# A hand-scheduled scan, attention and expert kernel: larger steps for the side work, a smaller pace for the experts, and a folded weight product two banks at a time

## The chip, the cores and the metric

The kernel runs on one core of a Trainium2 chip. The metric is the device time of one execution in microseconds (us), the median of several runs. The engines are named PE (TensorE), DVE (VectorE), ACT (ScalarE), POOL (GpSimd) and SP (SyncE, which issues nearly all DMAs here).

## The reference

Four images of 384 channels and 32 by 32 pixels, all float32. Layer 0 is a selective state-space scan after a group norm; layer 1 is causal attention and a mixture of four experts.

```python
x = x + L0(_gn(x))                 # group norm, projections, scan, norm, gelu
t = _to_tokens(x)                  # (4, 1024, 384)
t = t + attn(_ln_t(t), Wq, Wk, Wv) # causal, one head of 384
t = t + ffn(_ln_t(t), ...)         # gate; every expert 384 -> 1536 -> 384, top 2 kept

# in L0, for each of 4 directions, 384 channels, 16 states, over 1024 positions:
dA = jnp.exp(dtt[..., None] * A)
h = h * dA + (dtt * ut)[..., None] * bt[:, :, None, :]
y = jnp.einsum('bkdn,bkn->bkd', h, ct)

# in attn:
wei = softmax(where(causal, q @ k.T * scale, -inf));  out = wei @ v
```

## The kernel before

**Ticks.** The scan is cut into 768 units, 192 an image, each of 128 rows (32 channels by 4 states) and 1024 positions. The program is written out by hand as a loop over ticks, one unit a tick: ACT makes the decay `da` (`decay`, L554), DVE the product `v` (`front`, L561) and the scan `h` (`middle`, L567), POOL multiplies `h` by the output row (`back`, L584), and every fourth tick PE sums four units over their states into `y` with eight matmuls (`row`, L609). Each engine takes its instructions strictly in the order of this loop; there is no other scheduler.

**Work beside the scan.** Everything else is in generators that yield when they want to go on: `("wait", n)` is n ticks later, `("pe", n)` says that matmuls worth n units have been issued, `("inner", 0)` asks to be continued in the next tick ahead of its scan (`unpark`). At the end of every tick `go_on` (L1376) deals out TensorE time:

- `spare` grows by `pace` a tick, at most to `pace`.
- Every generator of the list `side` is stepped with a budget of 1.0. It goes on until its budget is used up or it waits, so a step that issues more than 1.0 ends its turn. What it used is taken from `spare`.
- What is left goes to the first generator of `waiting`, as long as `spare` is positive.

`side` holds `fold` (once, from tick 192), `finish` (the norm, gelu and sum that end layer 0 of an image), `ready` (the norm and the gates ahead of the experts, for each half image) and `skip`. `waiting` holds `behind(b)`, one for each image: it waits for `finish(b)`, then runs `attention` at a pace of 4.4 and `experts` at a pace of 3.3. So while image b + 1 is scanned, image b's attention and experts run on PE. `preparation(b)` (group norm, projections `pxd` and `pdt` to the step sizes, and `du` on DVE, L441) runs ahead of it, a step of 1.0 a tick.

**The pieces that the change touches.** `layernorm` (L639 on) issues the mean matmuls `mu` (L652), subtracts on DVE (L660), squares on ACT, sums with `var` (L679), takes the root on ACT (L687) and the reciprocal on DVE (L692), spreads it with `rb` (L698) and multiplies on DVE (L708). `finish` calls it with 1024 columns (tiles `..._l0`), `ready` with 512 (`..._ff`). `scaled_tokens` is attention's own norm (`var_at`, `rs_at`, `rb_at`, result `axn`). `fold` makes, from the weights, the centred product of query and key (`pwt`, `pg`) and the centred value weight (`pwv`), and stores both in DRAM (`g_d`, `wv_d`); `attention` loads them for every image (`wg_`, `wv_`). `experts` issues `ph` (L1272), moved by ACT and put through gelu in place (L1257, L1261), and `fy` (L1297), weighted and summed on DVE (L1306, L1309).

**Buffers.** `banks` are four PSUM banks of 512 columns (two during image 1), `slots` eight SBUF buffers of 4 KB a partition; `take` waits for one in steps of a tick. `pools["ht"]` has two buffers, which `fold`, the attention's `qt` and `vt` and the experts' `ht` share.

Of the kernel before, what the change touches and what calls it, by code (L numbers as in the profile page):

```python
# [8 lines left out]
F32 = mybir.dt.float32  # L9
AF = mybir.ActivationFunctionType  # L10
ALU = mybir.AluOpType
# [4 lines left out]
P = 128  # L16
B = 4
C = 384
M = C // P
HW = 32  # L20
L = HW * HW
# [21 lines left out]
AHEAD = 5  # L43
SLOTS = 8
PACE_A = 4.4
PACE_E = 3.3


@with_exitstack
def hybrid_kernel(  # L50
# [22 lines left out]
    nc = tc.nc  # L73
# [17 lines left out]
    pools = {  # L91
        "st": first.enter_context(tc.tile_pool(name="stp", bufs=2)),
        "v": first.enter_context(tc.tile_pool(name="ps_v", bufs=2, space=PSUM)),
        "pm": ps_m,
    }
# [22 lines left out]
    class Shared:  # L118
# [20 lines left out]
        def give(self, *names):  # L139
# [3 lines left out]
    banks = Shared(  # L143
        FIRST_BANKS,
        lambda i, name: (ps_m if i < FIRST_BANKS else pools["pm"]).tile(
            [P, 512], F32, tag=f"pm{i}", name=name
        ),
        0,
    )
    slots = Shared(  # L150
        SLOTS, lambda i, name, *shape: slotp.tile(list(shape), F32, tag=f"s{i}", name=name), 1
    )
# [7 lines left out]
    ident = const.tile([P, P], F32, tag="ident", name="ident")  # L160
    make_identity(nc, ident)
    mean_w = const.tile([P, P], F32, tag="mean_w", name="mean_w")
# [87 lines left out]
    scale = float(C) ** -0.5  # L250
# [465 lines left out]
    def fold():  # L716

        extra = pools["a0"].tile([P, M, L], F32, tag="a0", name="w_extra")
        extra = extra.rearrange("p m l -> p (m l)")
        vs = extra[:, : 2 * M * C].rearrange("p (j c d) -> p j c d", j=2, c=M)
        centre = extra[:, 2 * M * C : 2 * M * C + 2 * P].rearrange("p (j d) -> p j d", j=2)
        nc.sync.dma_start(vs[:, 0], wv.rearrange("(c p) d -> p c d", p=P))
        for same in range(2):
            nc.vector.scalar_tensor_tensor(
                centre[:, same, :], ident, float(same), mean_w, ALU.mult, ALU.subtract
            )  # L730
        def square(name):
            t = pools["ht"].tile([P, M, L], F32, tag="ht", name=name)
            t = t.rearrange("p m l -> p (m l)")[:, : 2 * M * C]
            return t.rearrange("p (j c d) -> p j c d", j=2, c=M)

        raw = square("w_raw")
        for j, w in enumerate((wq, wk)):
            nc.sync.dma_start(raw[:, j], w.rearrange("(c p) d -> p c d", p=P))
        wt = square("w_t")
        yield "wait", 2  # L740
        for j in range(2):
            for d in range(M):
                ps = yield from banks.take(f"pwt_{j}_{d}")
                for c in range(M):
                    for o in range(M):
                        nc.tensor.matmul(
                            ps[:, c * P : (c + 1) * P], raw[:, j, o, d * P : (d + 1) * P],
                            centre[:, int(o == c), :], start=(o == 0), stop=(o == M - 1),
                        )
                yield "wait", 1  # L750
                nc.scalar.copy(wt[:, j, d, :], ps[:, :C])
                banks.give(f"pwt_{j}_{d}")
        g = square("g_s")[:, 0]
        for m in range(M):
            ps = yield from banks.take(f"pg_{m}")
            for d in range(M):
                nc.tensor.matmul(
                    ps[:, :C], wt[:, 0, d, m * P : (m + 1) * P], wt[:, 1, d, :],
                    start=(d == 0), stop=(d == M - 1),
                )  # L760
            yield "wait", 1
            nc.scalar.activation(g[:, m, :], ps[:, :C], AF.Copy, scale=-scale)
            banks.give(f"pg_{m}")
        yield "wait", 1
        nc.sync.dma_start(g_d, g)
        for m in range(M):
            ps = yield from banks.take(f"pwv_{m}")
            for c in range(M):
                nc.tensor.matmul(
                    ps[:, :C], centre[:, int(c == m), :], vs[:, 0, c, :],  # L770
                    start=(c == 0), stop=(c == M - 1),
                )
            yield "wait", 1
            nc.scalar.copy(vs[:, 1, m, :], ps[:, :C])
            banks.give(f"pwv_{m}")
        yield "wait", 1
        nc.sync.dma_start(wv_d, vs[:, 1])
        folded.append(1)


# [119 lines left out]
    def scaled_tokens(b, yb):  # L900

        sqs = []
        for c in range(M):
            sq = yield from slots.take(f"sq_at_{b}_{c}", P, L)
            nc.scalar.activation(sq, yb[:, c, :], AF.Square)
            sqs.append(sq)

        var = yield from banks.take(f"var_at_{b}")
        for o, src in ((NH * P, [yb[:, c, :] for c in range(M)]), (0, sqs)):
            for h in range(NH):  # L910
                for c in range(M):
                    for q in range(4):
                        k = h * 512 + q * P
                        nc.tensor.matmul(  # L914
                            var[32 * q : 32 * (q + 1), o + h * P : o + (h + 1) * P],
                            mean_w[:, :32], src[c][:, k : k + P],
                            start=(c == 0), stop=(c == M - 1), tile_position=(0, 32 * q),
                        )
                yield "pe", 1.0
        slots.give(*[f"sq_at_{b}_{c}" for c in range(M)])  # L920
        rs = one.tile([P, NH, P], F32, tag=f"rs{NH}", name=f"rs_at_{b}")
        flat = rs.rearrange("p h t -> p (h t)")
        nc.scalar.activation(flat, var[:, NH * P : 2 * NH * P], AF.Square)
        yield "inner", 0
        nc.vector.tensor_tensor(flat, var[:, : NH * P], flat, ALU.subtract)
        banks.give(f"var_at_{b}")
        nc.scalar.activation(rs, rs, AF.Sqrt, bias=eps)
        yield "wait", 1
        nc.vector.reciprocal(rs, rs)
        backs = []  # L930
        for h in range(NH):
            rb = yield from banks.take(f"rb_at_{b}_{h}")
            for q in range(4):
                nc.tensor.matmul(  # L934
                    rb[:, q * P : (q + 1) * P],
                    ident[:, 32 * q : 32 * q + 1].to_broadcast([P, P]), rs[:, h, :],
                    start=True, stop=True,
                )
            backs.append(rb)
            yield "pe", 1.0  # L940
        while b > 0 and b - 1 not in stored:

            yield "wait", 1
        xn = pools["a0"].tile([P, M, L], F32, tag="a0", name=f"axn_{b}")
        yield "inner", 0
        for h in range(NH):
            s = bass.ts(h, 512)
            nc.vector.tensor_tensor(
                xn[:, :, s], yb[:, :, s], backs[h].unsqueeze(1).to_broadcast([P, M, 512]), ALU.mult
            )  # L950
            banks.give(f"rb_at_{b}_{h}")
        return xn

    def attention(b, yb, fx0):

        alone = b == B - 1
        while not folded:
            yield "wait", 1
        gw_ = []
        for name, w in ((f"wg_{b}", g_d), (f"wv_{b}", wv_d)):  # L960
            ta = yield from slots.take(f"{name}a", P, 2, C)
# [1 line left out]
            tb = yield from slots.take(f"{name}b", P, C)  # L963
            nc.sync.dma_start(tb, w[:, 2, :])
            gw_.append((ta[:, 0, :], ta[:, 1, :], tb))
        xn = yield from scaled_tokens(b, yb)
        qt = pools["ht"].tile([P, M, L], F32, tag="ht", name=f"qt_{b}")
        vt = pools["ht"].tile([P, L // P, C], F32, tag="ht", name=f"vt_{b}")

# [384 lines left out]
    def step(g, budget):  # L1354

        if g in ended:
            ended.remove(g)
            return None
        while budget > 0 and until.get(id(g), -100) <= clock[0]:
            try:  # L1360
                what, n = next(g)
            except StopIteration:
                return None
            if what == "pe":
                budget -= n
            elif what == "inner":
                parked.append(g)
                until[id(g)] = clock[0] + 1
            elif what == "start":
                started.append(1)  # L1370
                break
            elif n > 0:
                until[id(g)] = clock[0] + n
        return budget

    def go_on():  # L1376
        spare[0] = min(spare[0] + pace[0], pace[0])
        for g in side[:]:
            left = step(g, 1.0)
            if left is None:  # L1380
                side.remove(g)
            else:
                spare[0] -= 1.0 - left
        while waiting and spare[0] > 0:
            left = step(waiting[0], spare[0])
            if left is None:
                waiting.pop(0)
                continue
            spare[0] = left
            break  # L1390
# [100 lines left out]
```

## Time and profile before

| | |
|---|---|
| median of 3 runs | 3749.89 us (3745.99 to 3752.34) |
| the profiled execution | 3747.14 us, its span 3745.0 us |
| mean granted PE clock | 0.932 |
| PE busy | 3350.6 us (89%) |
| DVE busy | 2961.6 us (79%) |
| ACT busy | 2085.8 us (56%) |
| first and last scan start | 50.3 us, 3078.5 us |

Busy times are shares of the whole span; the stages differ. Matmul records overlap, so that a busy PE need not be a full one. In the tables of waits, a line "DVE du L441 <- PE fy L1297: 15.2, 6, 6.7" says that DVE stood idle ahead of `du` for 15.2 us in 6 places, 6.7 at most, until PE's fy matmuls released it. In the lines by stretch, the columns are the stretch, its length, then busy us (and instructions) of PE, PE weight loads, DVE, ACT and POOL, the granted PE clock, the DMA share and GB/s.

### The profile page before, as it was taken

The page shows a single profiled execution, that of the slowest core. Times are in us where ns is not written, and L with a number is a line of the kernel's source. Part 1 is how long each engine was busy: PE and PEld are TensorE (multiplying, and loading weights), DVE is VectorE, ACT ScalarE, POOL GpSimd, SP SyncE. Part 2 cuts the span into 40 slices and gives each one's busy share as a digit, 9 for nine tenths or more (in the row PEclk, how much of TensorE's full clock was granted, in tenths as well). Part 3 has the DMA queues.
Part 4 walks back from the last instruction along what each step waited for, and adds up shares of the span by engine and source line. Part 5 has one row for each costly group of instructions (what it writes and reads, how often), then busy time and mean ns, then how long its engine had stood idle before and what let it go on. Part 6 is the DMA issues. An engine that isn't in the chain of part 4 may idle for free. (4 is left out here: it accounts for less than half of the span.)

```text
span 3745.0 us, 35189 instructions
## 1 busy us (share of the span) xinstructions
PE 3350.6 (89%) x11891; PEld 1529.0 (41%) x11891; DVE 2961.6 (79%) x2084; ACT 2085.8 (56%) x2832; POOL 1817.8 (49%) x776
## 2 busy tenths in 40 slices
PE   4666667789999999898999999889999998999999
PEld 1333333345333343344333344454344444544444
DVE  5999899988998998989998999999999982210000
ACT  4788888556666555566655555455554552412121
POOL 2777777555565565545555665455665650000000
PEclk7677777899999999999999999899999999999999
DMA  6665666645665756436666665455657551322321
GB/s 204 219 233 199 208 218 221 215 145 199 235 222 201 260 206 230 155 138 228 217 221 229 201 210 192 146 182 188 223 192 240 179 182 38 92 82 83 96 82 53
DMA packets 408019, 680.03 MB, mean 182 GB/s; under 512 B 33520, under 2 KB 279968, under 8 KB 407840
## 3 DMA queue, kind: packets, MB, share of 16 engines
q1 hardware_dynamic: 401632, 677.40, 53.0%
q8 instruction: 94, 1.54, 0.2%
q10 hardware_dynamic: 6208, 0.39, 0.1%
q14 instruction: 85, 0.70, 0.1%
HBM read 605.16 MB, written 72.55 MB: 181 GB/s over the span
## 5 line engine op out<-in xcount | busy, mean ns | idle before, releaser
L584 POOL TENSOR_TENSOR h<-h,bc 128x1024 f32<-128x1024 f32 x768 | 1816.7, 2370 | 1264.9 <-DVE v L561 1058.3
L567 DVE TENSOR_TENSOR_SCAN h<-da,v 128x1024 f32<-128x1024 f32 x768 | 1748.4, 2283 | 48.4 <-PE v L872 17.3
L554 ACT ACTIVATE da<-dt,a 128x1024 f32<-128x1024 f32 x768 | 886.5, 1162 | 868.1 <-DVE h L567 759.3
L1297 PE MATMUL fy<-ht,w 128*128 128x512 f32 x2304 | 1019.8, 599 | 7.5 <-ACT ht L1261 5.9
L1272 PE MATMUL ph<-fx,w 128*128 128x512 f32 x2304 | 1019.1, 598 | 3.8 <-DMA w<-in_w 2.9
L561 DVE TENSOR_TENSOR v<-du,bc 128x1024 f32<-128x1024 f32 x664 | 842.8, 1269 | 61.9 <-DMA du<-dts 25.9
L1297 PEld LDWEIGHTS fy<-ht,w 128*128 128x128 f32 x2304 | 435.6, 191 | 580.3 <-issue 551.0
L1272 PEld LDWEIGHTS ph<-fx,w 128*128 128x128 f32 x2304 | 433.4, 191 | 579.6 <-issue 529.5
L609 PE MATMUL y<-h,sel 128*32 128x512 f32 x3072 | 493.3, 657 | 91.2 <-POOL h L584 89.2
L1257 ACT ACTIVATE ht<-ph,b1s 128x512 f32<-128x512 f32 x384 | 257.9, 679 | 471.0 <-PE ph L1272 469.2
L1306 DVE SCALAR_TENSOR_TENSOR fy<-fy,b2s,tw 128x512 f32<-128x512 f32 x96 | 72.0, 750 | 423.0 <-PE fy L1297 423.0
L609 PEld LDWEIGHTS y<-h,sel 128*32 128x32 f32 x3072 | 96.6, 115 | 399.3 <-issue 220.3
L850 ACT ACTIVATE st<-turn,bt 128x128 f32<-128x128 f32 x832 | 244.2, 554 | 0.0
L872 PE MATMUL v<-ident,st 128*128 128x128 f32 x832 | 147.5, 337 | 86.2 <-DVE h L567 85.4
L1261 ACT ACTIVATE ht<-ht 128x3072 f32<-128x3072 f32 x64 | 176.9, 2764 | 0.8
L872 PEld LDWEIGHTS v<-ident,st 128*128 128x128 f32 x832 | 121.7, 175 | 127.7 <-DVE h L567 74.2
L554 ACT ACT_TABLE_LOAD x99 | 127.0, 1283 | 18.7 <-DMA dt<-dts 12.3
L425 PE MATMUL pdt<-xd,wdt 12*128 12x512 f32 x184 | 88.0, 813 | 45.7 <-ACT dt L433 22.6
L1079 PE MATMUL po<-pt,vt 128*128 128x256 f32 x480 | 102.8, 364 | 7.1 <-ACT pt L971 7.1
L1009 PE MATMUL ss<-axn,qt 128*128 128x512 f32 (+3 forms) x288 | 102.3, 503 | 3.9 <-ACT yb L1096 3.9
L1079 PEld LDWEIGHTS po<-pt,vt 128*128 128x128 f32 x480 | 90.4, 192 | 22.3 <-ACT pt L971 10.1
L1009 PEld LDWEIGHTS ss<-axn,qt 128*128 128x128 f32 x288 | 51.5, 196 | 47.1 <-issue 33.5
(208 smaller groups left out, 1612.3 us busy)
## 6 DMA issues: line engine op xcount, KB each, us to landing
bc<-rows SPq DMA_DIRECT2D x384, 512.0 KB, 4.7
w<-in_w SPq DMA_DIRECT2D x384, 384.0 KB, 6.0
dt<-dts SPq DMA_DIRECT2D x192, 512.0 KB, 4.5
du<-dts SPq DMA_DIRECT2D x192, 512.0 KB, 6.6
dts<-dt SPq DMA_DIRECT2D x48, 512.0 KB, 4.7
dts<-du SPq DMA_DIRECT2D x48, 512.0 KB, 5.3
fx<-t2d SPq DMA_DIRECT2D x12, 768.0 KB, 5.5
tw<-mkd SPq DMA_DIRECT2D x32, 256.0 KB, 6.2
```

The costliest lines, as they stand in the source:

```text
L554: u["decay"] = nc.scalar.activation(u["da"], spread["dt4", n], AF.Exp, scale=a4[:, g, u["q"] : u["q"] + 1])
L561: return nc.vector.tensor_tensor(u["v"], spread["du4", n], spread["bc", n][:, 0, :], ALU.mult)
L567: nc.vector.tensor_tensor_scan(u["h"][:, ::step], u["da"][:, ::step], u["v"][:, ::step], 0.0, op0=ALU.mult, op1=ALU.add,)
L584: product = units[n]["product"] = nc.gpsimd.tensor_tensor(h, h, spread["bc", n][:, 1, :], ALU.mult)
L609: units[n]["row"] = nc.tensor.matmul(y, sel, h, start=first, stop=last, tile_position=(0, jj * DJ))
L850: nc.scalar.activation(st[:, 4 * h + t, :].rearrange("p (d i) -> p i d", i=NI)[:, i, :], ps[h][:, t * P : (t + 1) * P], AF.Copy, scale=bt[ ...
L872: nc.tensor.transpose(u["v"][:, t * P : (t + 1) * P], st[:, t, u["j"] * P : (u["j"] + 1) * P], ident)
L1079: nc.tensor.matmul(pv[:, o:], vt[:, j, m * P : (m + 1) * P], pts[step][j // 4][:, j % 4, o:], start=(alone and j == 0), stop=(j == nj - 1),)
L1257: nc.scalar.activation(ht[:, f, :], ps, AF.Identity, bias=bias)
L1261: nc.scalar.activation(ht, ht, AF.Gelu)
L1272: nc.tensor.matmul(ps, tiles[n][:, c, (f % 2) * P : (f % 2 + 1) * P], xns[h][:, c, :], start=(c == 0), stop=(c == M - 1),)
L1297: nc.tensor.matmul(pss[m], tiles[n][:, f, :], hts[fh][:, f, :], start=(fh == 0 and f == 0), stop=(fh == 1 and f == FH - 1),)
```

## The change

The budget of a side generator's step goes from 1.0 to 3.0, and the experts' pace from 3.3 to 3.2. `fold` keeps its value weight and centring matrices in slots and not in attention's buffer `a0`, issues two banks of matmuls a tick and moves them a tick later, and stores both results at its end. For the first image, `attention` runs `scaled_tokens` before it waits for `fold` and before it loads the weights.

```diff
-PACE_E = 3.3
+PACE_E = 3.2
+BESIDE = 3.0
...
     def fold():
-        extra = pools["a0"].tile([P, M, L], F32, tag="a0", name="w_extra")
...
-        nc.sync.dma_start(vs[:, 0], wv.rearrange("(c p) d -> p c d", p=P))
...
         raw = square("w_raw")
         for j, w in enumerate((wq, wk)):
             nc.sync.dma_start(raw[:, j], w.rearrange("(c p) d -> p c d", p=P))
+        va = yield from slots.take("va", P, 2, C)
+        vb = yield from slots.take("vb", P, C)
+        centre = yield from slots.take("centre", P, 2, P)
+        wvs = wv.rearrange("(c p) d -> p c d", p=P)
+        nc.sync.dma_start(va, wvs[:, :2, :])
+        nc.sync.dma_start(vb, wvs[:, 2, :])
+        vs = (va[:, 0, :], va[:, 1, :], vb)
...
-        yield "wait", 2
-        for j in range(2):
-            for d in range(M):
-                ps = yield from banks.take(f"pwt_{j}_{d}")
-                for c in range(M):
-                    for o in range(M):
-                        nc.tensor.matmul(
-                            ps[:, c * P : (c + 1) * P], raw[:, j, o, d * P : (d + 1) * P],
-                            centre[:, int(o == c), :], start=(o == 0), stop=(o == M - 1),
-                        )
-                yield "wait", 1
-                nc.scalar.copy(wt[:, j, d, :], ps[:, :C])
-                banks.give(f"pwt_{j}_{d}")
-        g = square("g_s")[:, 0]
-        for m in range(M):
-            ps = yield from banks.take(f"pg_{m}")
...
-            yield "wait", 1
-            nc.scalar.activation(g[:, m, :], ps[:, :C], AF.Copy, scale=-scale)
-            banks.give(f"pg_{m}")
-        yield "wait", 1
-        nc.sync.dma_start(g_d, g)
...
+        def by_twos(what, jobs):
+            for n in range(0, len(jobs), 2):
+                some = jobs[n : n + 2]
+                while not banks.ready(len(some)):
+                    yield "wait", 1
+                names = [f"{what}_{n + i}" for i in range(len(some))]
+                moves = [f(banks.now(name)) for f, name in zip(some, names)]
+                yield "wait", 1
+                for move in moves:
+                    move()
+                banks.give(*names)
+
+        yield "wait", 2
+        pairs = [(j, d) for d in range(M) for j in range(2)]
+        yield from by_twos("pwt", [lambda ps, j=j, d=d: turned_weight(j, d, ps) for j, d in pairs])
+        both = square("g_s")
+        jobs = [lambda ps, m=m: product(m, ps) for m in range(M)]
+        yield from by_twos("pg", jobs + [lambda ps, m=m: centred(m, ps) for m in range(M)])
+        slots.give("va", "vb", "centre")
+        nc.sync.dma_start(g_d, both[:, 0])
+        nc.sync.dma_start(wv_d, both[:, 1])
+        yield "wait", 1
         folded.append(1)
...
     def attention(b, yb, fx0):
         alone = b == B - 1
-        while not folded:
-            yield "wait", 1
+        if b == 0:
+            xn = yield from scaled_tokens(b, yb)
+            while not folded:
+                yield "wait", 1
         gw_ = []
...
-        xn = yield from scaled_tokens(b, yb)
+        if b > 0:
+            xn = yield from scaled_tokens(b, yb)
...
         for g in side[:]:
-            left = step(g, 1.0)
+            left = step(g, BESIDE)
             if left is None:
                 side.remove(g)
             else:
-                spare[0] -= 1.0 - left
+                spare[0] -= BESIDE - left
```

More of the change, by code (lines that the diff above doesn't have):

```diff
@@ L716, in fold @@
     def fold():
-        extra = pools["a0"].tile([P, M, L], F32, tag="a0", name="w_extra")
-        extra = extra.rearrange("p m l -> p (m l)")
-        vs = extra[:, : 2 * M * C].rearrange("p (j c d) -> p j c d", j=2, c=M)
-        centre = extra[:, 2 * M * C : 2 * M * C + 2 * P].rearrange("p (j d) -> p j d", j=2)
-        nc.sync.dma_start(vs[:, 0], wv.rearrange("(c p) d -> p c d", p=P))
-        for same in range(2):
-            nc.vector.scalar_tensor_tensor(
-                centre[:, same, :], ident, float(same), mean_w, ALU.mult, ALU.subtract
-            )
         def square(name):
@@ L738, in fold, with turned_weight, product @@
             nc.sync.dma_start(raw[:, j], w.rearrange("(c p) d -> p c d", p=P))
-        wt = square("w_t")
-        yield "wait", 2
-        for j in range(2):
-            for d in range(M):
-                ps = yield from banks.take(f"pwt_{j}_{d}")
-                for c in range(M):
-                    for o in range(M):
-                        nc.tensor.matmul(
-                            ps[:, c * P : (c + 1) * P], raw[:, j, o, d * P : (d + 1) * P],
-                            centre[:, int(o == c), :], start=(o == 0), stop=(o == M - 1),
-                        )
-                yield "wait", 1
-                nc.scalar.copy(wt[:, j, d, :], ps[:, :C])
-                banks.give(f"pwt_{j}_{d}")
-        g = square("g_s")[:, 0]
-        for m in range(M):
-            ps = yield from banks.take(f"pg_{m}")
+        va = yield from slots.take("va", P, 2, C)
[5 more added lines that the diff above has]
+        vs = (va[:, 0, :], va[:, 1, :], vb)
+        for same in range(2):
+            nc.vector.scalar_tensor_tensor(
+                centre[:, same, :], ident, float(same), mean_w, ALU.mult, ALU.subtract
+            )
+        wt = square("w_t")
+        def turned_weight(j, d, ps):
+            for c in range(M):
+                for o in range(M):
+                    nc.tensor.matmul(
+                        ps[:, c * P : (c + 1) * P], raw[:, j, o, d * P : (d + 1) * P],
+                        centre[:, int(o == c), :], start=(o == 0), stop=(o == M - 1),
+                    )
+            return lambda: nc.scalar.copy(wt[:, j, d, :], ps[:, :C])
+        def product(m, ps):
             for d in range(M):
@@ L760, in fold, with centred @@
                 )
-            yield "wait", 1
-            nc.scalar.activation(g[:, m, :], ps[:, :C], AF.Copy, scale=-scale)
-            banks.give(f"pg_{m}")
-        yield "wait", 1
-        nc.sync.dma_start(g_d, g)
-        for m in range(M):
-            ps = yield from banks.take(f"pwv_{m}")
+            return lambda: nc.scalar.activation(both[:, 0, m, :], ps[:, :C], AF.Copy, scale=-scale)
+        def centred(m, ps):
             for c in range(M):
                 nc.tensor.matmul(
-                    ps[:, :C], centre[:, int(c == m), :], vs[:, 0, c, :],
+                    ps[:, :C], centre[:, int(c == m), :], vs[c],
                     start=(c == 0), stop=(c == M - 1),
                 )
-            yield "wait", 1
-            nc.scalar.copy(vs[:, 1, m, :], ps[:, :C])
-            banks.give(f"pwv_{m}")
+            return lambda: nc.scalar.copy(both[:, 1, m, :], ps[:, :C])
+        def by_twos(what, jobs):
[18 more added lines that the diff above has]
+        nc.sync.dma_start(wv_d, both[:, 1])
         yield "wait", 1
-        nc.sync.dma_start(wv_d, vs[:, 1])
         folded.append(1)
@@ L956, in attention @@
         alone = b == B - 1
-        while not folded:
-            yield "wait", 1
+        if b == 0:
+            xn = yield from scaled_tokens(b, yb)
+            while not folded:
+                yield "wait", 1
         gw_ = []
```

## The prediction

> **What bounds the kernel now.** I began with the page's slices: they show two regimes.
>
> ```profile
> PE   4666667789999999898999999889999998999999
> DVE  5999899988998998989998999999999982210000
> PEclk7677777899999999999999999899999999999999
> ```
>
> VectorE is at 9 until slice 32 (the scans end at 3078.5 us), then falls away while TensorE stays at 9. So there are two clocks: the 768 scan ticks, then what TensorE still has to do. Next, busy time by stretch: 80 ticks of the third image's experts, and the gap after the last scan.
>
> ```profile
> 2651.00:2959.00 308.00, 307.77 (x935) 124.04 (x934) 301.30 (x186) 167.70 (x155) 189.10 (x81) 1.00 0.64 216
> 3092.50:3143.90 51.40, 38.69 (x241) 21.86 (x237) 21.71 (x19) 15.01 (x18) 0.00 (x0) 0.87 0.20 69
> ```
>
> First line: VectorE is busy 301.3 of 308 us over 186 instructions, which leaves 36 ns an instruction: no wait, so it sets a tick of 3.85 us. TensorE reads as full too, so the two are nearly balanced. Second line: TensorE has 12.7 us idle in 51.4, and its clock falls to 0.87. Then the waits of VectorE from 675 to 3078 us (images 2 to 4 in the scan):
>
> ```profile
> DVE nb L1026 <- PE ss L1014: 17.0, 7, 9.5
> DVE du L441 <- PE fy L1297: 15.2, 6, 6.7
> DVE v L561 <- PE y L609: 11.1, 9, 3.7
> DVE du L441 <- PE ph L1272: 10.6, 3, 8.9
> DVE du L441 <- ACT dt L433: 5.1, 3, 2.6
> ...
> DVE sc L1130 <- PE pgate L1123: 2.9, 1, 2.9
> DVE red L1145 <- ACT sc L1143: 2.5, 2, 1.6
> DVE axn L948 <- PE rb_at L934: 2.3, 3, 1.1
> DVE rs_l L692 <- ACT rs_l L687: 1.8, 1, 1.8
> DVE rs_at L925 <- ACT rs_at L923: 1.6, 1, 1.6
> DVE fx L660 <- PE mu_ff L652: 1.4, 1, 1.4
> ```
>
> These are what a lighter TensorE can win: 30.9 us for du (the step-size projections that sit behind expert matmuls), 11.1 for the y rows, 18.8 for the row minima nb. Last, the chain that ended last, where image 4's first norm goes over into its attention:
>
> ```profile
> 3126.32 1.14 ACT yb L888
> 3127.49 1.22 DVE yb L893
> ...
> 3131.29 4.54 PE var_at L914 x80
> ...
> 3138.09 1.76 DVE rs_at L929
> 3139.99 2.06 PE rb_at L934 x8
> 3142.07 1.76 DVE axn L948
> 3143.88 15.72 PE pq L980 x36
> ```
>
> Until 3143.88 TensorE waits for the other engines, step by step; from there the chain is nearly all TensorE, to 3745.
>
> **What the Trainium skill says.** "Perfetto Trace Analysis", section "Tensor Engine Instruction (MATMUL, LD_WEIGHTS)": the end of a matmul in a profile is estimated, and VectorE and ScalarE are strict FIFO. The trace agrees on the first: a ph matmul shows 598 ns, while starts lie 429 ns apart, so I price TensorE by starts. The second is why a late TensorE stops the scans: du stands in front of the next scan on VectorE. "ScalarE: Activation LUTs", "What ACT_TABLE_LOAD costs": 1283 ns a table load; the row of 99 loads has the same mean. "TensorE: Matmul & The Clock Gate", "What's actually happening": after an idle window of about 3.4 us the array runs at half speed; the records of var_at above stand 213 ns apart by fours where the layernorm's var stands at 107 elsewhere, after such a gap.
>
> **Prices** (start to start at full clock; each fp32 matmul is two records): 512 columns 0.858 us, 384 columns 0.644, 256 columns 0.43, 128 columns 0.22, the eight y matmuls of a row 2.05, a projection matmul pdt 0.52. A unit of the pace (2.6 for three 512-column matmuls, 2.574 us) is 0.99 us.
>
> **The change part by part.**
>
> *Work moved.* The matmuls are the same. Their order in the changed program, with these prices, gives the TensorE time (before/after, us) of ticks 0-192: 380.5/380.5; 192-256: 232.2/247.8; 256-384: 497.5/489.7; 384-448: 241.2/243.0; 448-576: 495.3/480.6; 576-640: 233.7/233.7; 640-768: 487.7/472.2; after the last row: 626.4/647.0. So 20.6 us leave the scan for the end: 12 ph and 12 fy matmuls of image 3's last expert. The early fold puts 15.6 us more before tick 256, and the smaller pace takes it back by tick 397, where image 1's experts end in both.
>
> *The scan, du and y.* I set the TensorE sum against the VectorE sum (scan 2.28, product 1.27, and so on, each plus 35 ns) four ticks at a time, and carry over what TensorE is late. Summed over the four-tick groups of ticks 256-512 that hold projection matmuls this backlog is 45.0 us before and 26.2 after, 42% less: of 30.9 us of du waits, **-13.1**. Over all groups from tick 192 it is 225 and 157, 30% less: of 11.1 us of y waits, **-3.3**. In the attention stretches it stays (59 and 59), so nb **0**. From tick 640 no such wait is left to win: VectorE sets the tick. Bounds: all 42 us, or nothing.
>
> *New tight handoffs.* With a budget of 3, a side generator goes through its next step in the same tick. In a layernorm one tick of slack goes between var and the reciprocal, one or two between rb and the multiply, and, with 512 columns (ff), one between mu and the subtraction. Behind each waiting VectorE instruction stands the next scan, and behind that GpSimd's product and the row. In the scan there are 3 l0 (2 handoffs) and 6 ff (3): 24. Before has handoffs of such a distance: axn 2.3, rs_at 1.6, sc 2.9, red 2.5, 9.3 us over 18, so 0.52 each; 24 x 0.52 = 12.4, less rs_l and fx mu_ff that it already pays (3.2): **+9.2**. Bounds: 0 (TensorE early every time) and 40 (each waits 1.7, the mean of du and nb being longer).
>
> *The end.* Before, from the end of the last y (3092.5) to pq: 51.4 us. After, by its order: ph 5.1, mu 5.1, ph 2.6, wait for the squares 1.3, var 1.5, square root and 1.75 reciprocal with nothing between 2.5, rb 1.4, ph 2.6, fy 30.9, var_at 2.4 (its inputs are long done, full clock), then the chain to pq as before 8.1: 63.6, so +12.2. The 9 us hole before var_at is filled by fy. Against it: before, TensorE is 6.0 us late at the last row by the sums (the last product ends at 3083.3, y starts at 3090.6); after, 0; I take -5.5. In the ff norms of image 4, rb no longer waits (1.4) but var does (about 2): +0.6. Together **+7.3**. From there 601 us as before.
>
> *Costed at nothing.* Fold's two banks a tick: the ScalarE copies are as many, and TensorE is idle 1.1 us a tick in ticks 192-208, which takes 14.6 us more with 17 to spare; if not, the mu and rb of the first norm wait, a few us. The load of wq and wk goes ahead of wv on SP's queue; still 2 ticks. The loads of the product for image 1 now stand on SP's queue behind var_at (their slots come from it) and in front of pq; between lie a square root, a 1.75 us reciprocal, rb and a multiply, about 8 us at 3131-3144, against 6.0 us to land for a like w load; without that cover 0 to 6 us of TensorE, in a stretch where VectorE sets the time. The three extra slots until tick 201 leave prep its own.
>
> *Sum.* -13.1 - 3.3 + 9.2 + 7.3 = +0.1 on the profiled execution (3747.14, its span 3745.0), which lies 2.8 under the median of the runs, 3749.89. So 3750.
>
> **Rivals.** A measurement of this kernel can tell about 0.2%, 7.5 us, from no change.
> *The stalls go altogether* (faster): with the load at 0.96 of VectorE's instead of 0.98, all but a quarter of du and y goes, -31.5, and handoffs cost 0.2 each, +1.6; with the end's +7.3: -22.6, about 3727. For it: no projection group from 256 to 468 keeps more than 3 us of backlog, tick 412 apart. Against: groups 484 and 500 then hold 6.
> *Handoffs stop the scans* (slower): the bursts put mu and var behind a tick of expert matmuls, 1.5 us a time: 24 x 1.5 - 3.2 = 33, so +24, 3774. It decides from (7.5 + 9.1 + 3.2)/24 = 0.8 us a handoff. For it: nb, emitted one tick after its matmuls, once waited 9.5. Against: at turnovers rows start as soon as their products are there.
> *The pace does nothing* (no change): VectorE sets the tick anyway, so only the end counts, +7.3, 3757.
>
> **How the numbers follow.** The even trade, with the last rival at its edge, 0.36, its own range 3742 to 3757; faster 0.33; slower 0.31. The range 3726 to 3771 takes in the first rival and the slower one up to 1.4 us a handoff.
>
> **What would show it.** After: du <- PE and ACT dt together near 18 us instead of 31; ticks 640-768 no shorter; about 63 us between the last y and pq, with var_at right behind fy; about 9 us more waits at L660, L692, L708's places. Wrong if the scans end more than 15 us earlier or at all later than 3078, or if pq starts less than 8 us later after the last y than before.

## The result, and the profile after

The changed kernel takes **3795.9 us**, median of four runs (3794.5 to 3799.9), against 3750.4 for the kernel before beside it: ratio **1.0122** [1.0109, 1.0135], 45.5 us slower. The forecast was 3750, with a range of 3726 to 3771. The profiled execution is 3796.39 us, its span 3794.6 (before 3745.0: +49.6).

First, of the page's slices of the changed kernel, VectorE and TensorE's granted clock: a digit for each fortieth of the span.

```profile
DVE  6999899897999999978999999999999982210000
PEclk7777777798999999898999999999999999999999
```

VectorE's row has a 7 in slices 10 and 18, where images turn over; before, no slice of the scans but the first was under 8. The clock has an 8 in slices 10, 17 and 19, where it had a 9. Stretch by stretch, from the starts of the scans and of three operations of image 4:

| stretch | before, us | after, us | change |
|---|---|---|---|
| start to tick 192 | 675.3 | 677.0 | +1.7 |
| ticks 192-208, image 1's layer-0 norm beside `fold` | 74.9 | 90.1 | **+15.2** |
| 208-224 | 73.5 | 68.6 | -4.9 |
| 224-240, end of attention, experts begin | 66.7 | 87.2 | **+20.5** |
| 240-256 | 75.2 | 74.5 | -0.7 |
| 256-384, experts of image 1 | 530.1 | 513.0 | **-17.1** |
| 384-400 | 74.2 | 76.0 | +1.8 |
| 400-448, image 2's norms and attention | 217.8 | 239.7 | **+21.9** |
| 448-576, experts of image 2 | 519.3 | 505.6 | **-13.7** |
| 576-640 | 280.8 | 286.7 | +5.9 |
| 640-767 | 490.7 | 490.3 | -0.4 |
| last scan to the start of the last `y` | 13.4 | 6.6 | -6.8 |
| to image 4's `pq` | 51.9 | 68.9 | **+17.0** |
| to its first `ph` | 93.2 | 99.4 | +6.2 |
| to the end | 507.9 | 510.9 | +3.0 |

The experts' stretches did get shorter, by 31 us in two. Every turnover and the beginning of the tail got longer by more. The waits of VectorE from 675 to 3110 us in the changed kernel say on what:

```profile
DVE fx L661 <- PE mu_ff L653: 21.9, 6, 10.9
DVE v L562 <- PE y L610: 21.8, 10, 5.2
DVE nb L1042 <- PE ss L1030: 12.6, 7, 4.6
DVE fx L709 <- PE rb_ff L699: 11.0, 5, 3.5
DVE yb L709 <- PE rb_l L699: 9.3, 3, 7.2
DVE du L442 <- PE fy L1313: 8.8, 2, 5.2
DVE du L442 <- ACT dt L434: 5.7, 2, 3.9
...
DVE rs_l L693 <- ACT rs_l L688: 3.2, 1, 3.2
DVE rs_ff L693 <- ACT rs_ff L688: 3.1, 2, 2.4
```

The step sizes `du` wait 14.5 us where they waited 30.9. In their place stand the norms: mu 21.9, rb 11.0 and 9.3, the roots 6.3, together 48.5 us in 17 places; before, they waited 3.2 in two. What such a wait looks like is seen in order of time (start, length, instruction; in brackets the idle time ahead and its releaser), image 1 ahead of the scan of tick 240 in the changed kernel:

```profile
911.87 1.25 DVE L562 TENSOR_TENSOR v<-du,bc 128x1024 f32<-128x1024 f32 x1
...
913.30 2.74 PE L393 MATMUL pxd<-x,wx 128*128 128x512 f32 x6
...
915.88 2.74 PE L1288 MATMUL ph<-fx,w 128*128 128x512 f32 x6
...
918.45 2.74 PE L653 MATMUL mu_ff<-fx,mean_w 128*128 128x512 f32 x6
...
921.23 1.75 DVE L661 TENSOR_TENSOR fx<-fx,mu_ff 128x1536 f32<-128x1536 f32 x1 [8.11 <-PE mu_ff L653]
922.90 2.28 DVE L568 TENSOR_TENSOR_SCAN h<-da,v 128x1024 f32<-128x1024 f32 x1
```

mu is only 2.7 us of work, but when the subtraction reaches the head of VectorE's queue (911.87 + 1.25 = 913.1), TensorE still has six `pxd` and six `ph` records in front of it, 5.2 us. VectorE stands 8.1 us, and the scan behind the subtraction, which doesn't need mu, stands with it. In the kernel before, the same subtraction waited 1.4.

The 48.5 us are not spread evenly. This wait and one of 10.9 ahead of 1764.5, where two records of `pdt`, six of `ph` and a row of y lie between VectorE's standing still and mu, make 19.0 of mu's 21.9; the other four are 1.4 at most. The longest wait for rb, 7.2 ahead of 726.2, has mostly the fold's product `pg` in front of it on TensorE. Three places hold 26.2 of the 48.5.

The end, from the last y (3116.0) to pq, beside ticks 192-208, by stretch (columns as in the section on the profile before):

```profile
3116.00:3184.30 68.30, 59.06 (x284) 30.00 (x284) 21.77 (x19) 21.35 (x25) 0.00 (x0) 0.94 0.22 74
676.98:767.10 90.12, 63.58 (x411) 38.40 (x411) 77.10 (x49) 51.16 (x59) 37.61 (x16) 0.81 0.49 178
```

TensorE still idles 9.2 us on the way to pq, where it idled 12.7, and 20.4 us of work have been put in front (59.06 to 38.69 busy). In ticks 192-208 VectorE, 72.1 us busy in 74.9 before, idles 13.0 of 90.1. The chain that ended last shows the idle time of the end:

```profile
3126.49 2.59 PE ph L1288 x6
...
3129.69 3.22 ACT sq_l L673 x6
3132.93 1.28 ACT L688
3134.22 0.48 ACT rs_l L688
3134.73 1.76 DVE rs_l L693
...
3136.53 3.79 PE rb_l L699 x16
...
3143.57 30.90 PE fy L1313 x72
3174.47 2.80 PE var_at L927 x96
```

From 3129.1 to 3136.5 nothing of TensorE is in the chain: squares, a table load (1.28), root and reciprocal follow each other. TensorE has only var to do meanwhile (3.0 us, beside the squares), and stands 1.3 us ahead of it and 3.2 behind it. The 30.9 us of fy come only after.

### The profile page after: what moved, and what is told of

Same layout as the page of the kernel before. It is cut to its first block, busy times and chain, and to the rows that moved or that the text cites. A ratio compares the mean times of both kernels' runs of the same rounds, so it can differ in the third digit from the quotient of the medians.

```text
span 3794.6 us, 35203 instructions
## 1 busy us (share of the span) xinstructions
PE 3378.5 (89%) x11891; PEld 1539.5 (41%) x11891; DVE 2964.8 (78%) x2084; ACT 2081.0 (55%) x2831; POOL 1815.9 (48%) x776
## 4 chain that ended last, share of the span: by engine, by line
DVE 46%; PE 36%; ACT 6%; issue 5%; DMA 4%; POOL 1%; SPq 1%; DVEq 0%; POOLq 0%; ACTq 0%
DVE h L568 26%; DVE v L562 15%; PE ph L1288 10%; PE fy L1313 9%; PE y L610 3%; PE po L1095 2%; PE ss L1025 2%; DMA du<-dts 2%; PE pq L996 2%; PE pv L1007 2%; ACT st L863 1%; ACT da L555 1%; PE pxd L393 1%; DVE fy L1322 1%; DVE du L442 1%
## 5 line engine op out<-in xcount | busy, mean ns | idle before, releaser
L1322 DVE SCALAR_TENSOR_TENSOR fy<-fy,b2s,tw 128x512 f32<-128x512 f32 x96 | 72.1, 751 | 450.9 <-PE fy L1313 450.9
L885 PE MATMUL v<-ident,st 128*128 128x128 f32 x832 | 148.2, 338 | 89.7 <-DVE h L568 88.8
L555 ACT ACT_TABLE_LOAD x99 | 127.0, 1283 | 20.3 <-DMA dt<-dts 11.7
L1095 PE MATMUL po<-pt,vt 128*128 128x256 f32 x480 | 112.9, 390 | 10.8 <-ACT pt L987 10.7
L426 PE MATMUL pdt<-xd,wdt 12*128 12x512 f32 x184 | 83.4, 784 | 40.2 <-ACT st L863 15.5
L1325 DVE TENSOR_TENSOR fx<-fx,fy 128x512 f32<-128x512 f32 x96 | 66.0, 687 | 3.3
```

The costliest lines, as they stand in the source:

```text
L555: u["decay"] = nc.scalar.activation(u["da"], spread["dt4", n], AF.Exp, scale=a4[:, g, u["q"] : u["q"] + 1])
L885: nc.tensor.transpose(u["v"][:, t * P : (t + 1) * P], st[:, t, u["j"] * P : (u["j"] + 1) * P], ident)
L1095: nc.tensor.matmul(pv[:, o:], vt[:, j, m * P : (m + 1) * P], pts[step][j // 4][:, j % 4, o:], start=(alone and j == 0), stop=(j == nj - 1),)
```

## The experiments

The theory after the result: the budget issues a norm's matmuls and what reads them too close together, and VectorE stands behind TensorE's queue (the handoffs; A and H1 in the expectations). Its rivals: the smaller pace leaves more for the end than it wins (the pace; B); the new fold and the new order of image 1's attention cost (C, and E later on), be it that the fold's double steps collide with the first norm (the collision) or that the first experts come before their weights (the late weights; D); the larger step crowds matmuls into one tick, so that rows and step sizes behind them are late too (the bursts; H2). Each expectation was written ahead of its run. The runs come from several sessions, in which the median of the kernel before lies between 3748.0 and 3752.3; each ratio is to the kernel before in the same session, so runs are compared by their ratios.

### One part alone, one part undone

The kernel before with the new pace alone:

```diff
-PACE_E = 3.3
+PACE_E = 3.2
```

> Before with the experts' pace at 3.2 and nothing else. Theory A (the budget of 3.0 is what costs; the pace is a gain in the expert stretches that is partly paid back at the end): the stretches 256-384 and 448-576 get some 15 us shorter each, as in the changed kernel, the end 10 to 20 us longer: 3730 to 3745. Rival B (the pace itself costs, since VectorE sets the tick and 20 us of matmuls only move to the end): 3755 to 3765.

The kernel before with the new budget alone:

```diff
-            left = step(g, 1.0)
+            left = step(g, 3.0)
...
-                spare[0] -= 1.0 - left
+                spare[0] -= 3.0 - left
```

> Before with the side generators' budget at 3.0 and nothing else (pace 3.3, the old fold). Theory A: nearly the whole loss is here, VectorE waits at the mean subtraction, the reciprocal and the last multiply of the norms grow to about 45 us, 3785 to 3805. Rival C (the loss is the new fold and the new order of image 1's attention, in ticks 192-256): 3750 to 3765.

The new fold and attention's new order alone, with the old pace and budget:

```diff
-PACE_E = 3.2
-BESIDE = 3.0
+PACE_E = 3.3
+BESIDE = 1.0
```

> Before with the new fold (two banks a tick, results stored together) and image 1's norm ahead of the wait for it, budget 1.0, pace 3.3. Theory A: within 8 us of before, 3742 to 3758. Rival C: ticks 192-256 alone lose about 30 us, 3775 to 3785.

The changed kernel with the old budget:

```diff
-BESIDE = 3.0
+BESIDE = 1.0
```

> The changed kernel with the budget back at 1.0: new fold and pace 3.2. Theory A: the waits at the norms go, 3725 to 3750. Rival B: 3755 to 3770; rival C: 3780 or more.

Measured:

| | median, us | ratio to before |
|---|---|---|
| pace alone | 3771.7 | 1.0056 [1.0039, 1.0073] |
| budget alone | 3770.1 | 1.0048 [1.0035, 1.0060] |
| fold and order alone | 3762.5 | 1.0031 [1.0020, 1.0041] |
| changed, budget 1.0 | 3785.1 | 1.0089 [1.0074, 1.0104] |

**Each part alone is a loss**, and the three, 0.56 + 0.48 + 0.31 = 1.35%, nearly add up to the whole's 1.22%. No single culprit. The expectations missed: the first three runs lie outside every range that was set for them, and the fourth lies where the fold's theory had put it (3780 or more), though the fold alone is at 3762.5 and not in that theory's 3775 to 3785.

*The pace.* Its last scan starts 8.4 us earlier (at 3070.1), but from there to the end it takes 40.2 us more (its profiled execution, 3778.7, is 7 us above its median). By the order of its program, at the prediction's prices, 672.7 us of matmuls stand behind the last row, against 626.4; the traces show 108 more records of ph and fy there. The stretch from the last y to pq, in the kernel with the new pace alone:

```profile
3079.37:3170.26 90.89, 83.04 (x346) 39.76 (x345) 23.31 (x21) 28.32 (x32) 0.00 (x0) 0.99 0.24 77
```

83.04 us of TensorE work in 90.9 stand there against 38.69 in 51.4: what the scan didn't get done is paid nearly in full, 39.5 us for 44.4. In the changed kernel the budget takes some of it back (647.0 behind the last row; with budget 1.0, 667.5), and even so costs 10.8 us net in its company. The changed kernel with budget 1.0 also shows that the norms' waits are the budget's: they are 10.0 us there and not 48.5, and the last scan starts 25.3 us earlier, of which the longer end takes back 13.4.

*The fold.* With the new fold and order alone, ticks 240-256 take 23.7 us more, ticks 256-384 then 11.8 less. TensorE in the kernel with the fold alone, in order of time:

```profile
898.58 5.49 PE L1288 MATMUL ph<-fx,w 128*128 128x512 f32 x6 [6.88 <-DMA w<-in_w]
```

The first experts wait 6.9 us for their weights, and their first six records then take twice the usual 2.74. ScalarE (ACT), which moves ph, stood 12.0 us for them, and the decay of the next scan stands behind that move.

### Which handoff of the norms

The budget alone with a tick of slack behind all three (`mu`, `var`, `rb`), with one behind `mu` alone, and with a budget of 2.0, at which mu's 2.6 still ends the step. The first two are on top of the budget alone, the third is in its place:

```diff
             mus.append(mu)
             yield "pe", 2.6
+        yield "wait", 1
         yield "inner", 0
...
             yield "pe", 1.0
+        yield "wait", 1
         slots.give(*[f"sq_{name}_{c}" for c in range(M)])
...
             backs.append(spread_)
             yield "pe", 1.0
+        yield "wait", 1
         yield "inner", 0
```

> Before with budget 3.0, and in the layernorm one tick of wait put back behind the mu, the var and the rb matmuls, so that VectorE and ScalarE read them as many ticks later as in before. Theory H1 (the budget costs because VectorE reads a tick too soon): waits at the subtraction, the reciprocal and the multiply fall from 33 us back under 8, 3743 to 3757. Rival H2 (it costs because the matmuls of side work and experts fall into one tick and everything behind them is late, rows and du as well): 3763 to 3775.

The first of these three lines alone:

> Before with budget 3.0 and only the tick of wait behind the mu matmuls put back; var and rb stay tight. With H1 the price goes by the wait: the subtraction had 21.9 of the 33 us of new waits in the run with budget 3.0 alone, so about two thirds of its 18 us come back: 3755 to 3763. If var and rb cost as much by what they hold up, 3765 or more.

```diff
-            left = step(g, 1.0)
+            left = step(g, 2.0)
...
-                spare[0] -= 1.0 - left
+                spare[0] -= 2.0 - left
```

> Before with budget 2.0: the mu matmuls (2.6) still end a step, so the subtraction keeps its tick; var and rb of the half-image norms lose theirs. H1: as in the run with only mu's tick put back, within 5 us of it, 3753 to 3763. H2 (bursts): between before and budget 3.0, as the bursts are: about 3760, not to be told from H1 here.

Measured: three waits 3755.1, 1.0012 [1.0005, 1.0019]; mu alone **3748.6, 0.9996** [0.9987, 1.0004]; budget 2.0 3752.4, 1.0002 [0.9994, 1.0011]. The wait for mu_ff, first with the budget alone, then with the slack behind mu:

```profile
DVE fx L660 <- PE mu_ff L652: 21.9, 5, 9.0
...
DVE fx L661 <- PE mu_ff L652: 7.3, 2, 4.7
```

14.6 us less, and the last scan starts 17.0 us earlier. One tick behind mu takes back the whole net cost of the larger budget, and so does a budget too small to go past mu. **The mu handoff is what makes the budget a loss**; slack behind the other two as well brings nothing more (ratio 1.0012 against 0.9996). Not everything is mended: with mu's tick the last scan still starts 10.4 us later than before, and the end is 8.3 shorter, for 36 fewer records of ph and fy stand behind the last row. Nor do these runs part the handoff fully from the bursts, since a tick of slack also spreads the matmuls; but the rows' waits do not fall with it (23.4 us with the budget alone, 26.8 with mu's tick), the step sizes' by about 6.

The same in the changed kernel, all three waits, then mu alone (the edits as above):

> The changed kernel with the same three ticks of wait. By its order 657 us of matmuls are left behind the last row instead of 647. H1: some 25 us less than the changed kernel's turnovers, 10 us more at the end, 3775 to 3785. H2: 3795 to 3805.

> The changed kernel with one tick of wait put back behind the mu matmuls of the norms and nothing else; by its order 644 us of matmuls stay behind the last row, as in the changed kernel (647). If the mu tick is most of the budget's price in the changed kernel too, 3774 to 3782; if the rest of its turnovers (first norm beside the fold, row minima, projections) is what costs there, 3788 or more.

Measured: 3788.4, 1.0109 [1.0094, 1.0124], and **3773.1, 1.0057** [1.0042, 1.0072]. mu's tick alone takes the loss from 1.22% to 0.57%, about half. Its waits of VectorE, 675 to 3102 us, have no mu_ff line any more:

```profile
DVE v L562 <- PE y L610: 19.0, 6, 4.7
...
DVE fx L710 <- PE rb_ff L700: 7.3, 2, 5.0
DVE yb L710 <- PE rb_l L700: 7.1, 2, 6.5
```

At the end the extra tick gives image 4's norm cover: twelve fy records, 5.15 us of its chain, stand between mu and `var` now where TensorE stood, and from the last y's start to pq are 62.9 us and not 68.9. With all three waits most of this is lost again: in the scans du waits 28.1 us for `dt` from ScalarE (20.5) and for ph, a gate reduction waits 12.6 once, and by program order 657.3 us stand behind the last row (644.4 with mu alone). That slower norms push the experts into the end fits; that it is all of the 0.52% between the two runs isn't shown.

### The pace the other way, and the first experts

The kernel before with pace 3.4:

> Before with the experts' pace at 3.4: by its order 616 us of matmuls behind the last row instead of 626, and 510 and 505 in ticks 256-384 and 448-576 instead of 498 and 495. If the pace only moves matmuls between the scan and the end, the end is some 10 us shorter at most (the hole ahead of var_at stays), and the expert stretches, where VectorE had waited for du, 10 to 20 us longer: 3750 to 3765. If TensorE has room there (VectorE sets the tick), 3738 to 3746.

Measured: 3754.1, 1.0011 [1.0002, 1.0020]. In its profiled execution, 5 us above its median, the last scan starts 14.9 us later and the rest is 2.3 shorter. So neither neighbour of 3.3 is better for the kernel before.

A hold of four ticks ahead of image 1's experts, in the kernel with the fold alone, in the changed kernel and in the kernel before:

```diff
+        if b == 0:
+            yield "wait", 4
         yield from experts(b, both[:, 0], (fx0, both[:, 1]))
```

> The new fold and order alone (budget 1.0, pace 3.3), and image 1's experts held for 4 ticks, so that they begin at the tick of before. Theory D (the new fold costs 10 us because image 1's experts then begin while image 3's group norm and projections hold the DMA queue, and TensorE stands 7 us for the first weights): ticks 240-256 come back from 98.9 to about 76 us, 3746 to 3754. Rival E (the fold itself, or the attention's earlier start, costs): stays at 3760 or more.

> The changed kernel with image 1's experts held for 4 ticks. Theory D: the 20 us that ticks 224-240 lose go down, as in the run of the new fold alone, against some 10 us more matmuls at the end (657 us instead of 647): 3775 to 3795. Rival: the loss there is only that of the tight norms, then no less than 3795.

> Before with image 1's experts held for 4 ticks, nothing else. The new fold with this hold was at 3740. If the hold alone does that (the norm and gates of the second half image are through before the experts' matmuls come), 3737 to 3745; if the earlier attention is needed to pay for the 4 ticks, 3748 to 3765.

Measured: fold with hold **3740.2, 0.9976** [0.9966, 0.9986]; changed with hold 3802.1, 1.0133 [1.0116, 1.0149]; before with hold 3744.4, 0.9981 [0.9972, 0.9990]. With the fold alone the hold mends the turnover (ticks 240-256 +3.7 instead of +23.7) and keeps the gain after it (-13.9), as the late weights would have it for that kernel: its first experts wait 1.1 us for weights. But it also helps the kernel before, where no stretch shows such a loss, and it doesn't help the changed kernel (3802.1 lies where the rival of its expectation was put), which has late weights too (its first ph at 901.64 waits 4.55 us, and a row queued behind it stops VectorE for 5.2). There the hold takes 7.6 of the 20.5 us off ticks 224-240, but ticks 576-640 lose 4.9 more and the way to pq 6.0 more, and by program order 657.3 us stand behind the last row instead of 647.0, twelve matmuls of experts more. So late weights cost time in both; that the hold fails to pay in the changed kernel because the matmuls it delays end up behind the last row fits these numbers, and isn't shown apart. Why the hold helps the kernel before is open: its profiled execution (3749.5) is among its longest and shows no gain.

### Put together

The changed kernel with mu's tick, the hold and pace 3.3; the same with 3.4; and the first with the budget at 1.0 until the fold is done:

> The changed kernel with the pace back at 3.3, the mu tick back and image 1's experts held for 4 ticks: 611 us behind the last row. If the three faults add up as they did singly (pace 21, mu tick 18, early experts 11), what is left is the gain of the shorter end: 3733 to 3748. If they don't add up, 3755 or more.

> The same with the pace at 3.4: 606 us behind the last row, 12 to 15 us more in each of the two expert stretches. If a larger pace only shifts matmuls, within 8 us of the run at 3.3; if VectorE's waits for the projections come back, 8 to 15 us longer.

```diff
-            left = step(g, BESIDE)
+            budget = BESIDE if folded else 1.0
+            left = step(g, budget)
```

> The run with pace 3.3, mu tick and hold, and the budget kept at 1.0 until the fold is done, so that image 1's first norm keeps its old ticks beside the new fold. If the 14 us that ticks 192-208 lost in every run with both the new fold and budget 3.0 (and in none with one of them) come from that norm's reciprocal and multiply standing behind the fold's matmuls, these ticks come back from 88.8 to about 76 us and the whole to 3745 to 3753. If it is something else in the two together, 3757 to 3763.

Measured: 3760.5, 1.0024 [1.0014, 1.0034]; 3767.5, 1.0041 [1.0026, 1.0056]; **3740.1, 0.9980** [0.9971, 0.9988]. The repairs don't add up to the 3733 to 3748 that was hoped for. The first two kernels still lose 14 us in ticks 192-208. Neither part does that alone: there, the budget alone loses 1.6 us (5.4 with mu's tick), the fold alone 0.8. Waits of VectorE between 674 and 765 us, first the kernel with mu's tick, hold and 3.3:

```profile
DVE yb L710 <- PE rb_l L700: 6.5, 1, 6.5
```

then with the small budget beside the fold (a root's wait of 3 to 4 us stands in both):

```profile
DVE yb L710 <- PE rb_l L700: 0.8, 1, 0.8
```

The stretch falls from 88.8 to 79.1 us and the kernel from 1.0024 to 0.9980. So **fold and norm collide only when both take large steps in the same ticks**; rb's wait is 5.7 of the 9.7 us. Ticks 208-224 give 4.7 of it back. Most of the rest of the gain lies in ticks 224-256, 12.5 us less; by what path isn't shown. This version and the fold with the hold are both 0.2% faster than the kernel before, and of one size.

## Why the prediction was wrong, point by point

No change was forecast, and the kernel got 45.5 us slower. The step that failed is the one called *New tight handoffs*: +9.2, from 24 x 0.52. The norms' waits grew from 3.2 to 48.5, by **+45.3**. The 24 places were the right ones, and 17 of them show a wait; the price was not: 48.5 over 24 is 2.0 us each, and what costs is a few deep ones, three with 26.2. The 0.52 came from the waits of axn, sc, red and rs_at. Two of these, red and rs_at, wait for ScalarE and not for TensorE, so they could say nothing of a queue on TensorE; the mu handoff had 5.2 us of pxd and ph in front of it where the text above shows it. The rival *Handoffs stop the scans* named just that ("behind a tick of expert matmuls") with 1.5 us a time, and its deciding point of 0.8 was passed; it got 3774 and a share of the 0.31. What is slower still, beyond 3774, comes from the other terms:

- **du -13.1**: measured -16.4. Right, and it shows where it should, in ticks 256-384 (-5.1) and 448-576 (-13.8). (As printed, 42% of 30.9 is 13.0, and the parts of the end add up to 63.5; neither slip matters.)
- **y -3.3**: measured +10.7, the wrong sign. In the experts' stretches and after tick 640 the rows' waits did fall, by 3.2; at the turnovers they grew by 13.9. A sum over four-tick groups does not see a row behind a ph that is itself late for its weights, as the one that cost 5.2. With budget 1.0 the turnovers' rows wait about as long (17.4 us in all, against 21.1), so most of this isn't the budget's.
- **nb 0**: -1.7. Right. Other small waits on the scan's side fell by 12.6. With du, y and the norms, -16.4 + 10.7 - 1.7 + 45.3 - 12.6 = 25.3 of the 30.2 us by which the last scan starts later (3108.8 against 3078.5).
- **The end +7.3**: from there to pq +10.2 where 6.7 was said. The row was on time, as said, and var_at does stand right behind fy. The stretch from y to pq took 68.4 us instead of 63.6. Of the missing 4.8, 4.5 lie between two ph groups, 11.2 us for 6.7: squares done 3.8 after ph and not 1.3, rb 3.79 and not 1.4, and a table load of 1.28 that stands in line and was left out of this sum. The Trainium skill, "ScalarE: Activation LUTs", "What ACT_TABLE_LOAD costs", prices the load at 1283 ns, as here; it adds a drain of about 1380 ns to each switch, which this trace doesn't show: the load starts 0.02 us after the last square, and the root 0.01 after the load.
- **From pq "601 us as before"** with +0.6: measured +9.1. Of it 6.2 lie up to the first ph. The granted clock there is 0.94, before 1.00, and 99.4 x 0.94 = 93.4 is close to the 93.2 of before. In all 18 traces this stretch, times its granted clock, comes to between 92.4 and 94.4 us. In the changed kernel the clock is at 0.50 from 3254.2 to 3261.0 and from 3271.3 to 3274.7. Shortly before each, TensorE had a hole: 1.85 us where var waited for the squares of a half-image norm, 1.08 where the gates waited for its multiply. These are handoffs too. That var would wait "about 2" was in the prediction; the slower clock after it was not. Only the three runs with budget 3.0 and no slack in the norm have these holes, and they take 98.0 to 99.4 us; the other 15 take 92.4 to 95.6.
- **Costed at nothing, the fold beside the first norm**: "if not, the mu and rb of the first norm wait, a few us". It is 15.2 in ticks 192-208 less 4.9 given back, and the last pair of runs shows the wait for rb to be part of it. That the first experts' weights come late once attention is earlier was not in the prediction at all.
- **Ticks 640-768 no shorter**: right (-0.4).

The pace wasn't a separate term, only the 20.6 us "that leave the scan for the end". That figure holds for the changed kernel. But the pace alone moves 46.3, for scans that end 8.4 us earlier: a trade that the sum never set against itself, and alone no smaller a loss than the budget. The rival *The pace does nothing* put its end at +7.3, for which the run of the pace alone shows +40.

The signs that were set out beforehand did tell: "wrong if the scans end at all later than 3078" came true, and the "about 9 us more waits" at the norms' places came out as 45. One did not: pq starts 17.0 us later after the last y, and the bound was 8.

## What to carry to other kernels

Price a handoff by what stands in front of its producer in the other engine's program order, and not by what other handoffs happen to cost: here that was anything from nothing to 11 us. Count the queued work place by place. A larger step in a hand-made interleave also takes away the distance that the small step's end had given to each handoff; give that distance back where the producer's queue is deep; here one tick in one place did better than three ticks in three. And work that a smaller share pushes behind the last unit of the bounding engine was paid nearly in full there, 40 us for 46, so set the two sums against each other before counting the stalls that go.

## What the runs showed of the hardware

With the fold alone, after TensorE had waited 6.88 us for weights, its next six ph records took 5.49 us, where six take 2.74 elsewhere (starts 0.853 us apart, and then 0.429): a late weight costs nearly three more than its wait. The Trainium skill, "TensorE: Matmul & The Clock Gate", "What's actually happening", which the prediction used for var_at, has the array at half speed after an idle window of about 3.4 us, and the run agrees. var_at agrees too: right behind fy, as in the changed kernel, its groups of four start 0.109 us apart, where they started 0.213 apart behind the holes of the kernel before.

Shorter holes can do it as well, and there the measurements go beyond that window. Between pq and the first ph of image 4, 15 of the traces have the same hole of 2.2 us in TensorE's work; in nine of them the granted clock is at 0.50 for 3.4 us right after it, which is 1.7 us lost, and in six, the kernel before among them, it stays at 1.00. What decides between the two isn't shown.
